# Edge sums of the last three node tiles by accumulating indirect DMAs, the order check taken out of the head, and the half blocks moved forward

## The chip, the cores and the metric

The kernel runs on one core of one Trainium2 chip. The metric is the device time of one launch in microseconds (us). One core has five engines that run side by side and wait for each other by semaphores: TensorE (PE, with its weight loads shown apart as PEld), VectorE (DVE), ScalarE (ACT), GpSimd (POOL) and SyncE (SP). SP issues nearly all plain DMAs; POOL issues the indirect ones, whose rows are picked by a list of indices in on-chip memory.

## The reference, cut to what matters

There are 3125 nodes with 256 features and 103,125 directed edges, sorted by destination: each of 50,000 drawn pairs in both directions, and a loop on each node. A node so has about 33 incoming edges.

```python
xn = layernorm(x)
agg = segment_sum(xn[src], dst, num_segments=N)          # the edge sums
h = relu(agg @ W_rel + b_rel + xn @ W_root)
gates = h @ W_ih.T + b_ih + b_hh                         # i, f, g, o; f is not used
h_lstm = sigmoid(o) * tanh(sigmoid(i) * tanh(g))
x = x + h_lstm @ W_fc + b_fc + mix(xn)                   # mix: 8 heads, linear attention
x = x + moe(layernorm(x))                                # 8 experts, top 2, 256 -> 1024 -> 256
```

## The kernel before, in words

The nodes are cut into T = 25 tiles of P = 126 rows. The kernel is one long program with stages that overlap a little.

**Head.** `norm` normalizes the nodes in five batches and stores them in `xn_dram`; `root` makes xn @ W_root for seven groups of tiles (`CUTS`). Beside it the generator `find` looks up the edges. Nodes are grouped by D = 6 (NG = 525 groups, GQ = 5 columns of GP = 105). For each group, five scans over the firsts of 128-edge rows (L258) and two rounds of indirect DMAs (`near` L266, `both` L281) bring its 256 edge slots; DVE turns them into a key (target within the group and source tile) and a row (source within its tile); L305 and L306 check that the edges are sorted, a matmul with ones (L311) adds up what is `wrong`, and `off`, made from that, is added to the keys (L325) so that nothing matches if the check fails. Then `rowT` and `keyT` hold the lists turned by PE.

**Edge stage.** The 3150 target columns are cut into chunks of AC = 252 (twelve, and a last one of 126). For each chunk, `build` makes an adjacency block from the lists: DVE compares (L382: `hr` and `hk`), PE multiplies the one-hot pairs (L388), ACT copies out (L390), 18 columns a step, 14 steps (`bank`) a chunk. Then 100 matmuls (L671: 25 source tiles, two halves of features, `hi` and `lo` parts of xn) sum the neighbours into `aggT`, which ACT copies at L679. While chunk c is multiplied, the blocks of chunk c+1 are built. The dictionary `queue` hangs the steps of the mixer (`fetch`, `means`, `differences`, `squares`, `sums`, `normed`, `products`) behind given banks, batch b from chunk 2b on. SP clears `xs_dram` in four fills (L698), after chunks 0, 2, 4 and 6. After the edge stage, `tc.If(total > 0)` holds a slow path for unsorted or overfull edges, which isn't entered with these inputs.

**Node stage.** `chunk(t0, t1, pending)` takes three or four tiles at a time: `aggT` by W_rel (L951), the gates (L961, 12 groups of matmuls for each of four m), W_fc (L980), then the router. POOL adds the bias to `base` (L943) and scatters the rows to their experts' lists in `xs_dram` by indirect DMAs (L1092, "puts"), 8 for a chunk of four tiles. The router's end of one chunk (`pending`) is issued behind m = 1 of the next.

**Block stage.** 24 sure blocks of SB = 256 slots and HSURE = 4 half blocks of 128 go through the experts' two matmuls (L865, L889). Each block loads 2 MB of weights into two buffers. For a block, POOL gathers the output rows (`old`, L845), adds (L900) and scatters them back (L901); a gather waits for the scatters of the block before it, since they may touch the same rows. The list `jobs` sets the order; half blocks stand behind blocks 10, 14, 18 and 22:

```python
        for b in range(EARLY, SURE):
            jobs.append((b, False))
            if b >= NE and (b - NE) % HSURE == HSURE - 2:
                jobs.append(((b - NE) // HSURE, True))
```

The order on each engine is set by a scheduler from the program's order; `tc.issue_after(ins)` places what is written under it behind that instruction.

Of the kernel before, what the change touches and what calls it, by code (L numbers as in the profile page):

```python
# [17 lines left out]
N = 3125  # L18
# [18 lines left out]
D = 6  # L37
NG = NP // D
GQ = 5
GP = NG // GQ  # L40
SB = 256
# [24 lines left out]
def gps_layer(  # L66
# [61 lines left out]

    aggT = main.tile([128, KC, NP], F32, name="aggT")
    edges = ExitStack()  # L130
# [17 lines left out]
    raw = sp.tile([128, 2, NCP], I32, name="raw")  # L148
    firsts = sp.tile([GP, NCP], I32, name="firsts")

    behind = sp.tile([128, NCP], I32, name="behind")
    nc.vector.memset(behind[96:, :], FAR)
    wroot = gw.tile([128, KC, DH], F32, name="wroot")

# [4 lines left out]

    nc.sync.dma_start(firsts, dst[0:1, :].to_broadcast([GP, NCP]))  # L160
    nc.sync.dma_start(raw[:, 0, :], dst)
    nc.sync.dma_start(raw[:, 1, :], src)
    def load_batch(b):
# [16 lines left out]
    nc.gpsimd.iota(limit, pattern=[[D * GP, GQ]], base=0, channel_multiplier=D,  # L180
                   allow_small_or_imprecise_dtypes=True)
    ones = const.tile([128, 128], F32, name="ones")
    nc.vector.memset(ones, 1.0)
# [36 lines left out]
    def find():  # L220
# [33 lines left out]

        below = sp.tile([GP, GQ], F32, name="below")
        scr = sp.tile([GP, NCP], F32, name="scr", tag="ends", bufs=3)
        for q in range(GQ):
            nc.vector.tensor_scalar(scr, firsts, limit[:, q:q + 1], None, op0=OP.is_lt, op1=OP.add,  # L258
                                    accum_out=below[:, q:q + 1])
# [11 lines left out]
        for q in range(GQ):  # L271
            nc.vector.tensor_scalar(scr[:, :128], near[:, q, :, 0], limit[:, q:q + 1], None,
                                    op0=OP.is_lt, op1=OP.add, accum_out=below[:, q:q + 1])
# [13 lines left out]
        st_ = sp.tile([GP, GQ, GE], F32, name="st_", tag="near")  # L287
        full = sp.tile([128, GQ], F32, name="full")
        nc.vector.memset(full, 0.0)
        for q in range(GQ):  # L290
            nc.vector.tensor_scalar(key[:, q, :], key[:, q, :], limit[:, q:q + 1], None,
                                    op0=OP.subtract)
            nc.vector.tensor_scalar(st_[:, q], g_src[:, q], -(P - 1) / 2.0, 1.0 / P,
                                    op0=OP.add, op1=OP.mult)
            nc.vector.tensor_scalar(st_[:, q], st_[:, q], MAGIC, MAGIC, op0=OP.add, op1=OP.subtract)
            nc.vector.scalar_tensor_tensor(g_src[:, q], st_[:, q], -float(P), g_src[:, q],
                                           op0=OP.mult, op1=OP.add)
            nc.vector.tensor_scalar(full[:GP, q:q + 1], key[:, q, GE - 1:], D - 0.5, None,
                                    op0=OP.is_lt)
            nc.vector.scalar_tensor_tensor(key[:, q], key[:, q], float(T), st_[:, q],  # L300
                                           op0=OP.mult, op1=OP.add)

        wrong = const.tile([128, 2], F32, name="wrong")
        order = sp.tile([128, NCP], F32, name="order", tag="ends", bufs=3)
        nc.vector.tensor_tensor(order, raw[:, 0, :], behind, OP.is_gt)  # L305
        nc.vector.tensor_reduce(wrong[:, 0:1], order, AX.X, OP.add)  # L306

        pins.append(nc.vector.tensor_reduce(wrong[:, 1:2], full, AX.X, OP.add))
        yield
        pw = ps_tr()  # L310
        nc.tensor.matmul(pw[:, :2], ones, wrong, start=True, stop=True)  # L311
        total_f = const.tile([128, 1], F32, name="total_f")
        nc.vector.tensor_reduce(total_f, pw[:, :2], AX.X, OP.add)
        off = const.tile([128, 1], F32, name="off")
        nc.vector.tensor_scalar(off, total_f, 1.0, float(FAR), op0=OP.min, op1=OP.mult)
        nc.vector.tensor_copy(total_i, total_f)
        for q in range(GQ):
            pt = ps_tr()
            for o, of in enumerate((g_src, key)):
                for h in range(GH):  # L320
                    nc.tensor.transpose(pt[:, (o * GH + h) * GP:(o * GH + h + 1) * GP],
                                        of[:, q, h * 128:h * 128 + 128], ident[:GP, :GP])
            nc.scalar.copy(rowT[:, q * GP:(q + 1) * GP, :],
                           pt[:, :GH * GP].rearrange("p (h g) -> p g h", h=GH))
            key_ = nc.vector.tensor_scalar(  # L325
                keyT[:, q * GP:(q + 1) * GP, :],
                pt[:, GH * GP:2 * GH * GP].rearrange("p (h g) -> p g h", h=GH),
                off, None, op0=OP.add)
        pins.append(key_)


# [61 lines left out]

    cuts = [*range(0, NP, AC), NP]
    chunks = list(zip(cuts, cuts[1:]))
# [55 lines left out]
    then(evacs[-1], rounded, 4)  # L451
    found.close()

    parts = builds(A0, 0)
    for c, n, m in ((5, 3, 4), (6, 3, NB)):
        root(c, lambda: [next(parts) for _ in range(n)])
        for _ in range(m):
            next(parts, None)
    with tc.issue_after(pins.pop().ins):
        for b in range(T // TB):  # L460
            u = slice(b * TB, b * TB + TB)
            nc.vector.tensor_tensor(lo[:, u, :], xn[:, u, :], hi[:, u, :], OP.subtract)
    nodes.close()

    gl = ctx.enter_context(tc.tile_pool(name="gl", bufs=1, side="right"))
# [99 lines left out]
    def squares(b, h):  # L565

        if h == 0:
            dn = mp.tile([P, TB, KC, 132], F32, name="dn", bufs=1)
            nc.gpsimd.memset(dn[:, :, :, 128:], 1.0)
            std = stat.tile([P, nh, 1], F32, name="hstd", bufs=2)  # L570
# [67 lines left out]

    queue = {}
    nb_ = T // TB  # L640
    for b in range(nb_):
        for c, i, step, *of in (
# [3 lines left out]
                (3, 1, products)):  # L646
            queue.setdefault((2 * b + c, i), []).append((step, b, *of))

    with tc.tile_pool(name="odd", bufs=1) as op_:
        As = [A0, op_.tile([P, T, AC], F32R, name="A1")]  # L650
        for c, (d0, d1) in enumerate(chunks):
# [5 lines left out]
            def bank(i):  # L657
# [3 lines left out]
                with ExitStack() as queued:  # L661
                    for ins in built:
                        queued.enter_context(tc.issue_after(ins.ins))
                    for step, *of in queue.pop((c, i), ()):
                        step(*of)

            i = 0
# [12 lines left out]
            if c == 1:  # L680
# [6 lines left out]
                for load in loads:  # L687
                    tc.add_manual_dep(load.ins, last.ins.name, mybir.DependencyInfo(
                        mybir.DependencyClass.Sync, mybir.DependencyReason.DATA), reason="later")
            if c == 2 * nb_ + 1:  # L690
                mixed()
# [13 lines left out]

    total = nc.values_load(total_i[0:1, 0:1], min_val=0, max_val=128 * NCP + NG)
    with tc.If(total > 0):
        with tc.tile_pool(name="any", bufs=1) as ap_:
# [8 lines left out]
            with tc.For_i(0, NCP, 1) as g:  # L717
# [33 lines left out]
                    in_=sums, in_offset=None, compute_op=OP.add)  # L751
            for t0 in range(0, T, TQ):
                ts = range(t0, min(T, t0 + TQ))
                ag = ap_.tile([P, TQ, C], F32, name="ag")
                nc.sync.dma_start(ag[:, :len(ts), :], tiles_of(agg_dram, t0, t0 + len(ts)))
                for k in range(KC):
# [4 lines left out]
                    col = aggT[:, k, t0 * P:(t0 + len(ts)) * P]  # L761
                    nc.vector.tensor_tensor(col, pt[:, :len(ts) * P], col, OP.add)

# [4 lines left out]
    class Block:  # L768


        def __init__(self, b, fp, half=False, xs=None):
# [21 lines left out]
            if xs is None:  # L793
                xs = fp.tile([128, NH, ROW], F32, name="xs", bufs=4)[:, :self.nh, :]
                rows = nc.sync.dma_start(xs, xs_b.rearrange("(h p) c -> p h c", p=128))
# [38 lines left out]
        def fetched(self, early):  # L834
# [4 lines left out]
            with ExitStack() as queued:  # L839
# [4 lines left out]
                for h in range(self.nh):  # L844
                    get = nc.gpsimd.indirect_dma_start(  # L845
                        out=old[:, h, :], out_offset=None, in_=out[:most, :],
                        in_offset=self.rows_(h), bounds_check=most - 1, oob_is_err=False)
                    for put in written if early else (*written, *ends_of_base):
                        after(get, put)
# [4 lines left out]
        def parts(self, following=None, apart=False):  # L854
# [21 lines left out]
            for h in range(nh):  # L876
# [11 lines left out]
                for m in range(KF):  # L888
                    mm = nc.tensor.matmul(po, hf[:, m, 128 * h:128 * h + 128], self.w2[:, m, :],  # L889
                                          start=(m == 0), stop=(m == KF - 1))  # L890
                y = fp.tile([128, C], F32, name="y", bufs=2 if early else 4)
                nc.vector.tensor_tensor(y, po, self.b2s, OP.add)  # L892
# [36 lines left out]
    with tc.tile_pool(name="gnn", bufs=1) as hp, tc.tile_pool(name="rt", bufs=2) as rp:  # L929
        CT = TQ * P  # L930
        wrows = rp.tile([P, NE, C], F32, name="wrows", bufs=1)
        nc.sync.dma_start(wrows, wr_dram[None, :, :].to_broadcast([P, NE, C]))

        def chunk(t0, t1, pending):

            ts = range(t0, t1)
            nt = len(ts)
            n = nt * P
            tok = slice(t0 * P, t0 * P + n)

# [6 lines left out]
            for m in range(KH):  # L947
                ms = slice(128 * m, 128 * m + 128)
                pm = ps_mm()
                for k in range(KC):  # L950
                    nc.tensor.matmul(pm[:, :n], wrel[:, k, ms], aggT[:, k, tok],  # L951
                                     start=(k == 0), stop=(k == KC - 1))
# [3 lines left out]
            for m in range(KH):  # L956
# [12 lines left out]
                if m == 1:  # L969

                    with tc.issue_after(mm.ins):
                        for _ in pending:
                            pass
            yield
            xl = rp.tile([P, TQ, C], F32, name="xl")
# [255 lines left out]
    with tc.tile_pool(name="ffn", bufs=2) as fp:  # L1231

        jobs = []
        for b in range(EARLY, SURE):
            jobs.append((b, False))
            if b >= NE and (b - NE) % HSURE == HSURE - 2:
                jobs.append(((b - NE) // HSURE, True))
        now = Block(jobs[0][0], fp, jobs[0][1])
# [89 lines left out]
```

## Time and profile before

| | us |
|---|---|
| runs shown (3) | 1113.99, 1111.55, 1114.54; median 1113.99 |
| profiled execution, its own time | 1118.92 |
| its span, first to last instruction | 1117.1 |
| PE busy | 1049.5 (94%) |
| PE weight loads busy | 814.8 (73%) |
| DVE busy | 553.6 (50%) |
| ACT busy | 437.9 (39%) |
| POOL busy | 245.3 (22%) |
| mean granted TensorE clock | 0.977 |

The profile page lists busy times and groups of instructions: line, engine, operation, output and inputs, count, busy time, mean duration, and the idle time just before them with what ended it. Matmuls overlap in the pipeline, so the duration of one is longer than the distance to the next. The trace can also be asked for instructions in order of time, and for busy times in given windows; those answers give starts in us from the span's start. The profiled execution is 4.93 us above the median of the runs shown.

### The profile page before, as it was taken

To read this page: it belongs to the slowest core of one execution; us is meant where nothing else is said; L and a number is where in the kernel's file an instruction comes from. 1 tells how busy PE (TensorE), PEld (TensorE's weight loads), DVE (VectorE), ACT (ScalarE), POOL (GpSimd) and SP (SyncE) were. 2 spreads that over 40 slices of the span, in tenths; PEclk is the share of its full clock that TensorE was granted. 3 is DMA by queue.
4 is the path that set the end of the run, shared out by engine and by line. 5 is a ranking of instruction groups with operands and counts; after the bars stand their busy time and mean duration, and the time that the engine had idled before them with its cause. 6 is when DMAs were issued, how large, how long until landed. Compare 5 with 4: busy or idle time off the path is not lost. (4 is left out here: it accounts for less than half of the span.)

```text
span 1117.1 us, 15758 instructions
## 1 busy us (share of the span) xinstructions
PE 1049.5 (94%) x5620; PEld 814.8 (73%) x5620; DVE 553.6 (50%) x1760; ACT 437.9 (39%) x942; POOL 245.3 (22%) x290
## 2 busy tenths in 40 slices
PE   4789999999999999999999999999999999999991
PEld 2358989989998454545465656788888888888881
DVE  5667778688772148484848644472112222222210
ACT  4454746647641334242435334452222322222230
POOL 2110000000000101212121130344434434344353
PEclk8999999999999999999999999999999999999996
DMA  8842897956003211262122310147666766676740
GB/s 252 314 165 80 223 289 180 242 146 169 1 1 113 74 37 62 69 222 63 51 58 60 97 59 15 48 130 268 202 220 213 248 209 207 217 242 202 244 163 26
DMA packets 113583, 164.28 MB, mean 147 GB/s; under 512 B 8102, under 2 KB 95945, under 8 KB 113370
## 3 DMA queue, kind: packets, MB, share of 16 engines
q1 hardware_dynamic: 103584, 140.49, 40.7%
q0 software_dynamic: 9072, 21.87, 5.9%
q8 instruction: 47, 0.77, 0.3%
q10 hardware_dynamic: 840, 0.83, 0.2%
q14 instruction: 40, 0.33, 0.1%
HBM read 104.98 MB, written 59.06 MB: 147 GB/s over the span
## 5 line engine op out<-in xcount | busy, mean ns | idle before, releaser
L961 PE MATMUL ps_mm<-hT,wih 128*128 128x504 f32 (+1 forms) x672 | 260.2, 548 | 0.0
L961 PEld LDWEIGHTS ps_mm<-hT,wih 128*128 128x128 f32 x672 | 128.3, 192 | 127.7 <-issue 91.5
L865 PE MATMUL ps_mm<-xe,w 128*128 128x256 f32 (+1 forms) x896 | 185.3, 364 | 0.0
L889 PE MATMUL ps_o<-w,hf 128*128 128x256 f32 x832 | 184.9, 379 | 0.0
L671 PE MATMUL ps_o<-A,hi 126*128 126x252 f32 (+1 forms) x650 | 178.1, 307 | 0.0
L865 PEld LDWEIGHTS ps_mm<-xe,w 128*128 128x128 f32 x896 | 160.5, 190 | 20.2 <-issue 0.2
L889 PEld LDWEIGHTS ps_o<-w,hf 128*128 128x128 f32 x832 | 155.7, 190 | 19.9
L671 PE MATMUL ps_o<-A,lo 126*128 126x252 f32 (+1 forms) x650 | 162.7, 283 | 0.0
L867 ACT ACTIVATE hf<-ps_mm,sm 128x256 f32<-128x256 f32 (+1 forms) x160 | 72.7, 454 | 184.4 <-PE ps_mm L865 181.4
L390 ACT CAST A<-ps_mm 126x450 fp32r<-126x450 f32 x175 | 93.9, 539 | 104.0 <-PE ps_mm L388 102.4
L671 PEld LDWEIGHTS ps_o<-A,hi 126*128 126x128 f32 x650 | 126.4, 194 | 1.8 <-ACT aggT L679 1.7
L671 PEld LDWEIGHTS ps_o<-A,lo 126*128 126x128 f32 x650 | 126.6, 195 | 0.0
L382 DVE TENSOR_TENSOR hr<-two,rowT 128x756 bf16<-128x756 bf16 x175 | 95.9, 548 | 49.8 <-PE ps_mm L388 49.0
L388 PE MATMUL ps_mm<-hk,hr 128*126 128x150 bf16 x1050 | 103.7, 235 | 15.2 <-DVE hk L382 15.1
L382 DVE TENSOR_TENSOR hk<-two,keyT 128x900 bf16<-128x900 bf16 x175 | 108.9, 622 | 0.0
L388 PEld LDWEIGHTS <-hr 128*126 128x126 bf16 x1050 | 92.5, 139 | 21.0 <-DVE hk L382 19.4
L963 ACT ACTIVATE act<-ps_mm,bg 128x504 f32<-128x504 f32 (+1 forms) x84 | 53.1, 636 | 111.2 <-PE ps_mm L961 101.2
L892 DVE TENSOR_TENSOR y<-ps_o,b2s 128x256 f32<-128x256 f32 x52 | 22.1, 424 | 118.9 <-PE ps_o L889 72.6
L1092 POOL DMA_INDIRECT xs_dram<-rows,at_i x50 | 50.2, 1003 | 122.6 <-DVE at_i L1090 108.6
L1012 DVE SCALAR_TENSOR_TENSOR scr<-xl,wrows 126x256 f32<-126x256 f32 x152 | 72.3, 476 | 3.1
L845 POOL DMA_INDIRECT old<-out_dram,xs x52 | 53.8, 1034 | 84.8 <-issue 51.4
L943 POOL TENSOR_TENSOR base<-base,bfc 126x1024 f32<-126x1024 f32 (+1 forms) x7 | 15.4, 2208 | 235.8 <-DMA base<-in_x_dram 154.2
(265 smaller groups left out, 1049.8 us busy)
## 6 DMA issues: line engine op xcount, KB each, us to landing
w<-in_W_dram SPq DMA_DIRECT2D x56, 1024.0 KB
xs_dram<-blank SPq DMA_DIRECT2D x3, 7022.5 KB
xs_dram<-blank SPq DMA_DIRECT2D x1, 6757.5 KB
xs<-xs_dram SPq DMA_DIRECT2D x21, 265.0 KB
root_dram<-hr SPq DMA_DIRECT2D x8, 504.0 KB
root<-root_dram SPq DMA_DIRECT2D x4, 1008.0 KB
b2s<-in_b_dram SPq DMA_DIRECT2D x28, 128.0 KB
xn_dram<-xn SPq DMA_DIRECT2D x5, 630.0 KB
```

Source lines behind the costliest of these rows:

```text
L382: row = nc.vector.tensor_tensor(to[:, :m], two[:, :, :w, :].to_broadcast([128, m, w, GH]), of[:, g:g + m, None, :].to_broadcast([128, m, w ...
L388: mm = nc.tensor.matmul(pa[:P, i * DT:(i + 1) * DT], hr[:, i, :, h], hk[:, i, :, h], start=(h == 0), stop=(h == GH - 1))
L390: copy = nc.scalar.copy(A[:, :, c0:c0 + m * D], pa[:P, :m * DT].rearrange("p (d t) -> p t d", t=T))
L671: last = nc.tensor.matmul(pg[k][:, :n], of[:, t, 128 * k:128 * k + 128], A[:, t, :n], start=(t == 0 and of is hi), stop=(t == T - 1 and of ...
L845: get = nc.gpsimd.indirect_dma_start(out=old[:, h, :], out_offset=None, in_=out[:most, :], in_offset=self.rows_(h), bounds_check=most - 1, ...
L865: mm = nc.tensor.matmul(pm, self.w1[:, k, 128 * m:128 * m + 128], self.xe[:, k, :], start=(k == 0), stop=(k == KC - 1))
L867: nc.scalar.activation(hf[:, m, :], pm, AF.Gelu, bias=b1s[:, m:m + 1])
L889: mm = nc.tensor.matmul(po, hf[:, m, 128 * h:128 * h + 128], self.w2[:, m, :], start=(m == 0), stop=(m == KF - 1))
L961: mm = nc.tensor.matmul(pm[:, :n], wih[:, k, i, 128 * m:128 * m + 128], hT[:, k, :n], start=(k == 0), stop=(k == KH - 1))
L963: nc.scalar.activation(act[:, i, :n], pm[:, :n], AF.Tanh if gate == 2 else AF.Sigmoid, bias=bg[:, gate, m:m + 1])
L1012: nc.vector.scalar_tensor_tensor(scr, xl[:, i, :], 1.0, wrows[:, e, :], op0=OP.mult, op1=OP.mult, accum_out=lg[:, i, e:e + 1])
L1092: put = nc.gpsimd.indirect_dma_start(out=xs_dram[:, :], out_offset=bass.IndirectOffsetOnAxis(ap=at_i[:, i:i + 1], axis=0), in_=rows[:, i, ...
```

## The change

Four things are done together.

1. The edge sums of the last three tiles (TG = 3, 378 target columns) are no longer made by matmuls. The edge stage ends after 11 chunks of 252 (TA = 22 tiles), and `find` serves 480 groups in 4 columns of 120. A new generator `find_last` finds, for each node of the last three tiles, its first edge and up to J = 60 sources, in the same manner as `find`; slots that aren't the node's point at row N of `xn_dram`, which holds zeros. `adds` then issues 60 x 3 indirect DMAs, each of which adds 126 rows of `xn_dram` onto one tile's sums in `flat` on chip. Adds onto the same tile wait for one another. 81 of them stand on POOL's queue in the edge stage (from chunk 0, bank 11, on; 5 for every 8 banks), 99 in the node stage, 5 behind each m. `turned`, behind m = 2 of the chunk that ends at tile 22, transposes the sums by PE for the last chunk.
2. The check of the order, its matmul and `off` move from `find` to `find_last`; `off` goes into the sources instead of the keys. `find_last` runs in chunk 0: its scans behind the last build of the first block, the rest behind banks 4, 8 and 10.
3. The mixer's batches start at chunks 0, 2, 3, 5 and 6 instead of 0, 2, 4, 6 and 8, and the `dn` memset goes from POOL to DVE.
4. The half blocks stand behind blocks 4, 7, 10 and 13. `xs` has 5 buffers instead of 4, `y` 6 instead of 4, and the gathers join the group of DMAs that are ordered by hand only.

```diff
-NG = NP // D
-GQ = 5
-GP = NG // GQ
+TG = 3
+TA = T - TG
+GQ = 4
+GP = 120
+NG = GQ * GP
+JE = 64
+J = 60
...
-    aggT = main.tile([128, KC, NP], F32, name="aggT")
+    aggT = main.tile([128, KC, TA * P], F32, name="aggT")
+    flat = main.tile([128, TG * C], F32, name="flat")
+    acc = flat[:P].rearrange("p (m c) -> p m c", c=C)
+    accT = flat[:, :KC * TG * P].rearrange("p (k n) -> p k n", k=KC)
...
-        order = sp.tile([128, NCP], F32, name="order", tag="ends", bufs=3)
-        nc.vector.tensor_tensor(order, raw[:, 0, :], behind, OP.is_gt)
-        nc.vector.tensor_reduce(wrong[:, 0:1], order, AX.X, OP.add)
...
-        nc.tensor.matmul(pw[:, :2], ones, wrong, start=True, stop=True)
...
+    def find_last():
+        below = ep.tile([P, TG], F32, name="below2")
+        for m in range(TG):
+            scr = sp.tile([128, NCP], F32, name="scr2", tag="ends", bufs=3)
+            nc.vector.tensor_scalar(scr[:P], firsts[:P], node[:, m:m + 1], None, op0=OP.is_lt,
+                                    op1=OP.add, accum_out=below[:, m:m + 1])
...
+        for m in range(TG):
+            nc.gpsimd.indirect_dma_start(
+                out=near[:, m].rearrange("p e o -> p (e o)"), out_offset=None,
...
+        nc.vector.tensor_tensor(order, raw[:, 0, :], behind, OP.is_gt)
+        nc.vector.tensor_reduce(wrong[:, GQ:GQ + 1], order, AX.X, OP.add)
+        yield
...
+        for m in range(TG):
+            nc.vector.tensor_scalar(mine[:, m], both[:, m, :, 0], node[:, m:m + 1], None,
+                                    op0=OP.is_equal)
...
+        nc.tensor.matmul(pw[:, :GQ + 2], ones, wrong, start=True, stop=True)
...
+        nc.vector.tensor_scalar(mine, mine, float(N), off[:P], op0=OP.add, op1=OP.add)
+        nc.vector.tensor_scalar(source, mine, float(N), None, op0=OP.min)
+
+    def adds():
+        nc.gpsimd.memset(acc, 0.0)
+        for j in range(J):
+            for m in range(TG):
+                yield nc.gpsimd.indirect_dma_start(
+                    out=acc[:, m, :], out_offset=None, in_=xn_dram[:, :],
+                    in_offset=bass.IndirectOffsetOnAxis(ap=source[:, m, j:j + 1], axis=0),
+                    compute_op=OP.add)
...
-    cuts = [*range(0, NP, AC), NP]
+    cuts = range(0, TA * P + 1, AC)
...
-    for b in range(nb_):
+    queue = {(0, i): [(next, last_steps, None)] for i in (4, 8, 10)}
+    ADDS = 11
+    for b, c0 in enumerate((0, 2, 3, 5, 6)):
...
+                n = c * NB + i - ADDS
+                if n >= 0 and n * 5 // 8 > (n - 1) * 5 // 8:
+                    next(adding)
...
+        def turned():
+            for _ in adding:
+                pass
+            pts = [ps_tr() for _ in range(KC)]
+            for k in range(KC):
+                for m in range(TG):
+                    nc.tensor.transpose(pts[k][:, m * P:(m + 1) * P],
+                                        acc[:, m, 128 * k:128 * k + 128], ident[:P, :P])
+            for k in range(KC):
+                nc.scalar.copy(accT[:, k, :], pts[k][:, :TG * P])
...
+                for i in range(5):
+                    add = next(adding, None)
+                    if add is not None and i == 0:
+                        after(add, mm)
+                if m == 2 and t1 == TA:
+                    with tc.issue_after(mm.ins):
+                        turned()
...
-            if b >= NE and (b - NE) % HSURE == HSURE - 2:
-                jobs.append(((b - NE) // HSURE, True))
+            if (b - EARLY) % 3 == 1 and (b - EARLY) // 3 < HSURE:
+                jobs.append(((b - EARLY) // 3, True))
```

## The prediction

> **What bounds the kernel now.** I read the page's first two parts, then busy times with one window for each edge chunk (a chunk ends where ACT starts the first copy to `aggT`, L679: 116.2, 134.6, 157.5, 178.2, 200.6, 221.5, 242.9, 263.5, 286.0, 306.9, 326.7, 344.1, 355.5 us), then DVE and POOL in order of time.
>
> ```profile
> span 1117.1 us, 15758 instructions
> PE 1049.5 (94%) x5620; PEld 814.8 (73%) x5620; DVE 553.6 (50%) x1760; ACT 437.9 (39%) x942; POOL 245.3 (22%) x290
> PE   4789999999999999999999999999999999999991
> DVE  5667778688772148484848644472112222222210
> POOL 2110000000000101212121130344434434344353
> ```
>
> PE is the bound from slice 4 to the last; POOL is empty in slices 4 to 13, the edge stage, where DVE runs close behind PE.
>
> ```profile
> L388 PE MATMUL ps_mm<-hk,hr 128*126 128x150 bf16 x1050 | 103.7, 235 | 15.2 <-DVE hk L382 15.1
> ...
> core 0: us, PE busy (x) PEld busy (x) DVE busy (x) ACT busy (x) POOL busy (x), PEclk, DMA share, GB/s
> 116.20:134.60 18.40, 18.40 (x187) 18.14 (x186) 14.96 (x30) 15.96 (x56) 0.00 (x0) 1.00 1.03 270
> 134.60:157.50 22.90, 20.49 (x186) 19.71 (x185) 19.68 (x37) 9.53 (x20) 0.00 (x0) 0.93 1.08 287
> 157.50:178.20 20.70, 20.70 (x208) 20.49 (x206) 14.49 (x28) 16.13 (x57) 0.13 (x1) 1.00 1.12 281
> 306.90:326.70 19.80, 19.00 (x186) 18.16 (x185) 17.44 (x35) 9.50 (x20) 0.00 (x0) 1.00 0.01 2
> 326.70:344.10 17.40, 17.40 (x164) 17.20 (x164) 7.03 (x18) 4.46 (x10) 0.00 (x0) 1.00 0.00 1
> 344.10:355.50 11.40, 11.40 (x104) 11.40 (x102) 2.34 (x10) 0.65 (x3) 0.00 (x0) 1.00 0.49 183
> ```
>
> These are chunks 1, 2, 3, 10, 11 and 12. With nothing but builds and `differences` a chunk takes 18.4; with `products` 20.7, PE full; with `squares`, `sums`, `normed` and the next `means` 22.9, PE idle 2.4 beside DVE's 19.7; the same without `means` 19.8; with 7 builds and `products` 17.4; the half-wide one without builds 11.4.
>
> **The matmuls taken away.** Chunks 1 to 12 take 355.5 - 116.2 = 239.3. After the change there are chunks 1 to 10, and with the new starts of the batches each holds: 1 differences 18.4; 2 squares and means 22.9; 3 products and means 20.9; 4 squares 20.5 (19.8, and ACT now has differences too); 5 products, squares and means 23.5 (22.9, products mostly inside DVE's excess); 6 products 20.9; 7 squares 20.5; 8 products and squares 21.7; 9 products 20.6; 10 neither builds nor steps, 100 matmuls about 0.117 apart, 11.7. Sum 201.6: **-37.7**. Bounds -32 (0.8 more in seven mixed chunks) and -41 (mixed chunks at PE's own 20.7). The node stage multiplies the same columns, so nothing changes on PE there.
>
> **The search moved into chunk 0.**
>
> ```profile
> 5.31 1.05 DVE L258 TENSOR_SCALAR_CACHE_REDUCE scr<-firsts,limit 105x808 f32<-105x808 int32 x1 [3.07 <-DMA firsts<-in_dst_dram]
> ...
> 24.93 0.35 DVE L272 TENSOR_SCALAR_CACHE_REDUCE scr<-near,limit 105x128 f32<-105x128 f32 x1 [2.55 <-DMA near<-ends_dram,at_i]
> ...
> 51.80 1.01 DVE L305 TENSOR_TENSOR order<-raw,behind 128x808 f32<-128x808 int32 x1
> ...
> 66.03 0.16 DVE L313 TENSOR_REDUCE total_f<-ps_tr 128x1 f32<-128x2 f32 x1 [9.32 <-PE ps_tr L311]
> ```
>
> The order check leaves the head for nothing: after it DVE idled 9.32 for PE. What the head does lose on PE is the matmul L311 (0.3) and 4 of 20 list transposes (3.0 in all, so 0.6): **-1**, bounds 0 and -1.5. In chunk 0 DVE gains three scans at 1.10, order 1.0 and its reduce 0.9, two small casts 0.3: 5.5 in one piece, ahead of the first build for chunk 1; behind bank 4 three counts and one sum, 1.4; behind bank 8 three compares and a reduce, about 0.9 by the 0.35 of L272; behind bank 10 sums and sources, about 1.5. Together 9.3. DVE was free for 24.2 - 19.8 = 4.4 of 92.0 to 116.2, so 4.9 come out on PE. Three waits are new: DVE for `near2`, for `both2` and for its matmul on PE. All later builds queue behind them on DVE, and PE behind the builds. Banks come every 1.45 or so; a gather of three needs 2.7 of issue and 2.5 to 6.8 of landing (below) where four banks give 5.8. I take 2.1: **+7**, bounds +3 (scans inside the 2.64 that DVE idled at 99.25, waits hidden) and +13 (nothing hidden).
>
> **The adds.** No accumulating DMA ran before, so bounds come from plain indirect ones.
>
> ```profile
> 18.10 1.16 POOL L266 DMA_INDIRECT near<-ends_dram,at_i  x1 [1.02 <-DVE xn L336]
> ...
> 444.01 1.10 POOL L1092 DMA_INDIRECT xs_dram<-rows,at_i  x1 [15.87 <-DVE at_i L1090]
> 445.42 1.00 POOL L1092 DMA_INDIRECT xs_dram<-rows,at_i  x1 [0.30 <-issue]
> ...
> 1091.70 1.05 POOL L845 DMA_INDIRECT old<-out_dram,xs  x1 [2.26 <-issue]
> 1092.74 0.54 POOL L843 MEMSET old<- 128x512 f32 x1
> 1094.18 0.72 POOL L900 TENSOR_TENSOR old<-y,old 128x256 f32<-128x256 f32 x1 [0.89 <-DMA old<-out_dram,xs]
> ```
>
> Issues follow each other at 1.3. From issue to the waiting instruction, a gather takes 2.5 on a quiet queue (1091.70 to 1094.18) and 6.8 on a loaded one (18.10 to 24.93). Three adds to three tiles are in flight and the fourth waits for the first, so a round of three costs the larger of 3.9 and the landing: 3.9 below; above, 6.8 doubled for the second operand that an add must read, 13.6. I take 5, nearest the quiet rows, since from 265 on the queues are nearly empty. What can it wait for? 27 rounds stand in the edge stage, from about 115 to its end near 325: room for 7.8 each. In the node stage 33 rounds share POOL with `base` (2.2, L943) and 8 puts (10.4) for each 56.2 us chunk; PE's m steps pace them, a put waits until some 30 into the chunk for DVE's `at_i`, and 14 adds, 4.7 rounds, must fit from 41 to the next chunk's first m, 73: again 7 or so, and 40 us are spare before `turned`. So up to 7.5 a round the adds cost **0**; they hide beside PE. Beyond that PE stands at `turned`: 33 rounds times the excess, some 25 to 30 us for each us of landing.
>
> A rule that speaks against this: the puts above were issued every 1.3 while DVE was busy 35.7 of 56.2, longest 1.373 of 50, so I see no stop. The Trainium skill, "SBUF — State Buffer", "Who interferes with whom" and "A bandwidth-pool intuition that's wrong", holds that POOL can't write a DMA's descriptors while DVE works in a mode that takes their shared ports, and gives 3.1 us against 0.62 for such a DMA. If each issue took 3.1, a round would take 9.3 and the whole gain be lost.
>
> `turned` adds six transposes; eight records of that kind took 1.03 (41.57, L356), so twelve take **+1.5**, bounds 1.5 and 4 (wait for two PSUM buffers); the ACT copies (0.5 each) have a node chunk's end to hide in. For packets of the adds among fills and loads, and DVE's `dn` memset now waiting for `products`, I set **+2**, bounds 0 and +10 (a `q` load late behind a fill).
>
> **Half blocks.** PE takes 14.25 for a full block and 10.7 for a half wherever it stands, PE was never idle from 750 on, and weights keep coming at a DMA share of 0.7. The end can move: the last matmul ended at 1094.6, the last scatter was issued at 1106.5, since each gather waits for the block before. With the half block gone from the place before last, two full blocks' time of PE lets the chain catch up: from the scatter at 1078.3 to that at 1088.4 a full block took 10.1 against 14.25. But a half took 6.8 against 7.5, so little is won at the end: **0**, bounds -8 and +4. More `xs` and `y` buffers only allow more lag.
>
> **Sum.** -37.7 - 1 + 7 + 1.5 + 2 = -28.2. Span 1117.1 to 1089, the profiled execution's 1118.9 to 1090.7; that execution was 4.9 above the median, so the median 1114.0 goes to 1085.8.
>
> **Rivals.** (a) *The adds land late.* An add may read, sum and write back row by row. At 9 a round instead of 7.5, PE waits some 40 at `turned`: 1126, slower than before; it decides from about 8.5 on. For it: the doubled loaded row. Against: 2.5 quiet, and little traffic in the node stage. 0.11. (b) *DVE takes the bound in the edge stage.* Chunk 0 grows by 13 and mixed chunks wait for batches that now overlap: -32 + 13 + 1.5 + 8 - 1 = -10, so 1103; for it DVE's 19.7 of 22.9 in chunk 2. 0.16. (c) *The tail shortens too*: -8 beside the forecast, 1078. 0.12. (d) *The removal doesn't reach the end*, because the block stage, fed by the same gathers, takes it back: 1112. For it: 11.9 us of chain behind the last matmul; against: PE was never idle there. 0.03. The forecast has 0.58.
>
> **Numbers.** A measurement tells some 0.3%, 3.3 us. Range 1072 (c, and the better edge bound) to 1108 (b with its bounds); outside stay (a) and some of (d). Faster 0.86, same 0.03, slower 0.11, from (a).
>
> **What would show it.** Right: 11 L679 pairs, the last near 323; POOL busy with adds every 1.3 to 2 in threes; no PE idle before the six transposes; the node stage's chunks still 56.2. Wrong: PE idle there with a DMA onto `flat` as releaser; more DVE waits before L388's successor than 15.1; chunk 0 beyond 129.

## The result, and the profile after

The kernel after takes 1246.96 us (median of 4 runs, 1237.64 to 1257.0) against 1112.82 before: a ratio of 1.117, 95% interval [1.111, 1.123]. By the medians it is slower by 134 us. The ratio counts the fast runs alone and so leaves out the longest, 1257.0, which is the profiled execution, with a span of 1255.0. The page of after, the same rows as shown of before, and the groups of the adds (L394) and of the gate matmuls (L1052, L961 before):

```profile
span 1255.0 us, 15252 instructions
PE 1036.3 (83%) x5296; PEld 788.6 (63%) x5296; DVE 534.9 (43%) x1733; ACT 424.3 (34%) x918; POOL 559.7 (45%) x471
PE   4787999999789994693791760799999999999995
POOL 2104556677663344445435436602543343344444
L394 POOL DMA_INDIRECT flat<-xn_dram,source x180 | 309.4, 1719 | 319.3 <-DMA flat<-xn_dram,source 281.8
L1052 PE MATMUL ps_mm<-hT,wih 128*128 128x504 f32 (+1 forms) x672 | 274.1, 568 | 134.0 <-ACT act L1054 132.2
```

PE is busy 13.2 us less, but stands idle for 219 us of the span (68 before), two thirds of it in slices 16 to 26. POOL waited 281.8 us between its adds for an earlier add to land. Cut into stages (edge stage; the gap until the first gate matmul; node stage; block stage; the tail from the last matmul on), the profile shows where the loss lies. These are the gap and the node stage, first before, then after:

```profile
core 0: us, PE busy (x) PEld busy (x) DVE busy (x) ACT busy (x) POOL busy (x), PEclk, DMA share, GB/s
355.70:364.40 8.70, 7.09 (x16) 3.05 (x17) 2.10 (x5) 2.06 (x5) 0.00 (x0) 1.00 0.44 152
364.40:714.80 350.40, 345.87 (x1072) 193.31 (x1071) 194.06 (x808) 133.09 (x216) 63.51 (x56) 0.99 0.23 71
...
331.80:354.20 22.40, 8.82 (x17) 3.71 (x17) 2.12 (x5) 2.27 (x5) 15.72 (x10) 0.71 0.71 148
354.20:860.90 506.70, 360.68 (x1078) 198.98 (x1077) 195.16 (x808) 133.01 (x217) 221.12 (x155) 0.85 0.34 73
```

The lengths of these stages in all profiled executions, each read off in the same way (gap: last edge matmul to first gate matmul):

| kernel | edge stage ends | gap | node stage | block stage | tail | span |
|---|---|---|---|---|---|---|
| before | 355.7 | 8.7 | 350.4 | 379.8 | 22.5 | 1117.1 |
| after | 331.8 | 22.4 | 506.7 | 379.8 | 14.3 | 1255.0 |
| no adds (e1) | 330.8 | 8.4 | 351.1 | 379.7 | 14.3 | 1084.3 |
| order mended (e2) | 328.2 | 21.2 | 355.7 | 379.9 | 14.1 | 1099.1 |
| plain gathers (e3) | 330.2 | 8.6 | 437.2 | 379.8 | 14.5 | 1170.3 |
| before + half blocks (e4) | 354.5 | 8.0 | 347.2 | 379.8 | 15.6 | 1105.1 |
| 65 edge adds (e5) | 328.4 | 8.5 | 373.2 | 379.8 | 14.6 | 1104.5 |
| six tiles (e6) | 331.8 | 8.4 | 375.3 | 379.7 | 12.0 | 1107.2 |
| edge adds only (e7) | 330.1 | 15.5 | 349.5 | 379.7 | 12.0 | 1086.8 |
| three rows buffers (e8) | 331.5 | 13.9 | 493.6 | 380.1 | 14.3 | 1233.4 |
| six tiles, late sum (e9) | 332.0 | 8.4 | 351.5 | 379.8 | 13.4 | 1085.1 |
| 97 edge adds (e10) | 336.4 | 8.5 | 351.5 | 379.8 | 14.2 | 1090.4 |
| no waits for PE (e11) | 329.4 | 23.7 | 459.6 | 379.8 | 14.4 | 1206.9 |

From before to after: edge stage -23.9, gap +13.7, node stage +156.3, tail -8.2. Who waits in the node stage of after, from the lists of what DVE and PE waited for (engine, tile and line, releaser; us in total, times, longest):

```profile
DVE rows L1179 <- DMA xs_dram<-rows,at_i: 151.8, 4, 50.5
PE ps_mm L1052 <- ACT act L1054: 132.2, 4, 45.3
```

Four times DVE stood at the first write to a chunk's `rows` buffer, whose scatters (L1191, of the chunk two before) had not been issued. DVE's next gate product queues behind that, then ACT's, then PE: one case, in order of time on all engines:

```profile
488.72 1.59 POOL L394 DMA_INDIRECT flat<-xn_dram,source  x1 [0.30 <-issue]
490.62 1.04 POOL L1191 DMA_INDIRECT xs_dram<-rows,at_i  x1 [0.30 <-issue]
...
502.62 0.17 DVE L1179 COPY rows<-token 126x4 int32<-126x4 int32 x1 [33.24 <-DMA xs_dram<-rows,at_i]
...
509.31 0.68 DVE L1057 TENSOR_TENSOR act<-act 128x504 f32<-128x504 f32 x1
...
510.56 0.67 ACT L1054 ACTIVATE act<-ps_mm,bg 128x504 f32<-128x504 f32 x1
...
511.27 5.59 PE L1052 MATMUL ps_mm<-hT,wih 128*128 128x504 f32 x8 [27.32 <-ACT act L1054]
```

POOL issued its scatters without a pause once it came to them; it came late, because the adds ahead of them were slow. This is POOL in the node stage of after:

```profile
383.96 1.59 POOL L394 DMA_INDIRECT flat<-xn_dram,source  x1 [3.13 <-DMA flat<-xn_dram,source]
388.33 1.59 POOL L394 DMA_INDIRECT flat<-xn_dram,source  x1 [2.78 <-DMA flat<-xn_dram,source]
390.22 1.59 POOL L394 DMA_INDIRECT flat<-xn_dram,source  x1 [0.30 <-issue]
394.49 1.59 POOL L394 DMA_INDIRECT flat<-xn_dram,source  x1 [2.68 <-DMA flat<-xn_dram,source]
399.06 1.62 POOL L394 DMA_INDIRECT flat<-xn_dram,source  x1 [2.98 <-DMA flat<-xn_dram,source]
403.32 1.59 POOL L394 DMA_INDIRECT flat<-xn_dram,source  x1 [2.65 <-DMA flat<-xn_dram,source]
```

An add every 4.3 to 4.6 us, one in flight, and only the first of each five without a wait for its predecessor. The DMA packets say the same: the add issued at 394.49 has its last packet at 398.29, and the next is issued at 399.06. The order of the instructions on POOL, as built (a, b, c are adds onto the three tiles, P is a scatter, base the bias addition), shows why:

```
edge stage:  a b c a b c a b c ...
node stage:  b c b b base base a a a a a c c c c c b b b b b a a a a a base
             c c c c c b P P P P P P P P b b b a b a a a a c c c c c base ...
```

In the node stage five adds onto one tile stand in a row. Of the five behind an m only the first waited for a matmul; the scheduler was free to place the other four elsewhere (e2 takes that freedom away). With three tiles in turn, the adds that wait are onto a, c and b by turns, and from one of them up to the next onto the same tile lie five adds of that tile. Adds onto one tile must wait for one another, so there POOL pays the whole round trip each time.

### The profile page after: what moved, and what is told of

Its sections match the earlier page's. It is cut to its first block, busy times and chain, and to the rows that moved or that the text cites. A ratio compares the mean times of both kernels' runs of the same rounds, so it can differ in the third digit from the quotient of the medians.

```text
span 1255.0 us, 15252 instructions
## 1 busy us (share of the span) xinstructions
PE 1036.3 (83%) x5296; PEld 788.6 (63%) x5296; DVE 534.9 (43%) x1733; ACT 424.3 (34%) x918; POOL 559.7 (45%) x471
## 3 DMA queue, kind: packets, MB, share of 16 engines
q0 software_dynamic: 38080, 45.57, 18.6%
## 5 line engine op out<-in xcount | busy, mean ns | idle before, releaser
L394 POOL DMA_INDIRECT flat<-xn_dram,source x180 | 309.4, 1719 | 319.3 <-DMA flat<-xn_dram,source 281.8
L1052 PE MATMUL ps_mm<-hT,wih 128*128 128x504 f32 (+1 forms) x672 | 274.1, 568 | 134.0 <-ACT act L1054 132.2
L1052 PEld LDWEIGHTS ps_mm<-hT,wih 128*128 128x128 f32 x672 | 133.1, 201 | 274.4 <-ACT act L1054 136.5
L746 PE MATMUL ps_o<-A,hi 126*128 126x252 f32 x550 | 151.3, 307 | 0.6 <-ACT A L458 0.6
L746 PE MATMUL ps_o<-A,lo 126*128 126x252 f32 x550 | 138.0, 283 | 0.0
L458 ACT CAST A<-ps_mm 126x450 fp32r<-126x450 f32 x154 | 82.3, 538 | 85.7 <-PE ps_mm L456 81.5
L746 PEld LDWEIGHTS ps_o<-A,hi 126*128 126x128 f32 x550 | 106.5, 194 | 2.4 <-ACT aggT L754 1.3
L746 PEld LDWEIGHTS ps_o<-A,lo 126*128 126x128 f32 x550 | 106.7, 194 | 0.0
L456 PE MATMUL ps_mm<-hk,hr 128*126 128x150 bf16 x924 | 91.8, 235 | 16.1 <-DVE hk L450 15.7
L450 DVE TENSOR_TENSOR hk<-two,keyT 128x900 bf16<-128x900 bf16 x154 | 95.7, 622 | 0.0
L1058 ACT ACTIVATE act<-act 128x504 f32<-128x504 f32 (+1 forms) x28 | 16.2, 578 | 186.3 <-DVE act L1057 186.3
L980 POOL TENSOR_TENSOR old<-y,old 128x256 f32<-128x256 f32 x52 | 37.7, 725 | 86.4 <-DMA old<-out_dram,xs 62.4
```

The costliest lines, as they stand in the source:

```text
L394: yield nc.gpsimd.indirect_dma_start(out=acc[:, m, :], out_offset=None, in_=xn_dram[:, :], in_offset=bass.IndirectOffsetOnAxis(ap=source[: ...
L450: row = nc.vector.tensor_tensor(to[:, :m], two[:, :, :w, :].to_broadcast([128, m, w, GH]), of[:, g:g + m, None, :].to_broadcast([128, m, w ...
L456: mm = nc.tensor.matmul(pa[:P, i * DT:(i + 1) * DT], hr[:, i, :, h], hk[:, i, :, h], start=(h == 0), stop=(h == GH - 1))
L458: copy = nc.scalar.copy(A[:, :, c0:c0 + m * D], pa[:P, :m * DT].rearrange("p (d t) -> p t d", t=T))
L746: last = nc.tensor.matmul(pg[k][:, :n], of[:, t, 128 * k:128 * k + 128], A[:, t, :n], start=(t == 0 and of is hi), stop=(t == T - 1 and of ...
L980: nc.gpsimd.tensor_tensor(old[:, h, :], y, old[:, h, :], OP.add)
```

## The experiments

Theory A: the adds cause the loss, through POOL's queue; A1: through their order on it. Rivals B to L are named in the expectations.

**e1, without adds.** In `adds`:

```diff
-        for j in range(J):
+        for j in range(0):
```

> The 180 adds are left out, so the last three tiles' edge sums are zero; all else of the change stays (find_last, turned, the shorter edge stage, the half blocks). Theory A (the adds cause the whole loss, as POOL's queue): the time falls to what the recorded sum gives without them, 1080 to 1092 us, with node chunks of 56 us and no wait of DVE for the scatters' rows buffer. Rival B (find_last, the mixer's overlapped batches or the half blocks cost much of it): more than 1115 us.

Measured: 1085.24 us, ratio 0.973 [0.971, 0.976] to before. The adds cost 162 us, more than the whole loss; B falls. The rest of the change is worth 29.5 us (before took 1114.72 beside this run).

**e2, the order mended.** Behind an m:

```diff
-                    if add is not None and i == 0:
+                    if add is not None:
                         after(add, mm)
```

> All five adds behind an m wait for its matmul, not the first alone, so that the queue goes round the three tiles again; in the kernel after, its node stage has five adds onto one tile in a row. Theory A1 (the order on the queue makes each add wait out the round trip of the one before, 4.3 us each, and the scatters behind them come late): rounds of three fall from about 13 us to about 6, the waits of DVE for rows in the node stage (152 us) go to below 15, and the time falls to 1095 to 1115 us, with the wait of 12 to 18 us at the start of the node stage left. Rival C (an accumulating DMA is slow in itself, whatever its neighbours): rounds stay above 10 us and the time above 1200 us.

Measured: 1104.40 us, 0.992 [0.988, 0.995]: 143 us less than after by one condition. POOL's queue goes a b c again, and its node stage looks like this, beside the lines of after above:

```profile
373.00 1.59 POOL L394 DMA_INDIRECT flat<-xn_dram,source  x1 [0.30 <-DMA flat<-xn_dram,source]
374.89 1.59 POOL L394 DMA_INDIRECT flat<-xn_dram,source  x1 [0.30 <-issue]
376.79 1.59 POOL L394 DMA_INDIRECT flat<-xn_dram,source  x1 [0.30 <-issue]
378.68 1.79 POOL L394 DMA_INDIRECT flat<-xn_dram,source  x1 [0.30 <-issue]
```

A round of three takes 5.7 to 6.6, set by issue and by PE's pace; no wait for `rows` is left among the longest of the node stage. A1 holds, C falls. Of the 19 us to e1, 12.8 of the profiled spans are the gap before the gates.

**e3, plain gathers in the order of after.** `compute_op=OP.add` is dropped.

> The same 180 DMAs at the same places, but each overwrites its tile instead of adding (the sums are then only the last rows). Theory A1: the chain is made of issue and round trip, of which the packets' own 1.4 us is the smaller part; the time falls by at most 0.5 us for each of 99 adds, to 1195 to 1247 us. Rival C: an overwriting gather lands in 2.5 us or less after its issue as on the quiet queue of before; rounds fall below 8 us and the time to 1100 to 1130 us.

Measured: 1172.69 us, 1.052 [1.049, 1.054], between the two forecasts. An overwriting gather's issue is 1.00 against 1.59, and the adds of the node stage come every 3.9 instead of 4.6 us in the median; DVE still waits 85.7 for `rows`. So adding costs 0.6 of POOL's time for each DMA and nothing that can be seen in landing; the chain remains. The two runs differ in more than the adding, though: the plain gathers move the same bytes in fewer packets (20,800 on that queue against 38,080). POOL is also past the edge stage's 81 in time here (gap 8.6). A1's bound of 0.5 for each was too low, and it left the gap out.

**e4, the half blocks alone**, on the kernel before: the changed condition in `jobs`, `xs` bufs 5, `y` bufs 6 and the line with the group of gathers.

> The kernel before with nothing but the half blocks moved forward (behind blocks 4, 7, 10, 13), five xs buffers, six y buffers and the gathers in the hand-ordered group. The recorded prediction: no change, 1106 to 1118 us. Rival D (the block stage gains by it, as the kernel after's block stage is 394 us long against 404): 1102 to 1106 us, the last scatter nearer to the last matmul or the block stage's PE idle time smaller.

Measured: 1107.21 us, 0.993 [0.990, 0.996], some 7.5 below the 1114.72 of before beside it. The block stage is as long as ever; the tail is 15.6 instead of 22.5, and the last scatter is issued 4.8 after the last matmul instead of 11.9. The time lies within the 1106 to 1118 that the recorded "no change" allowed and just above D's 1102 to 1106, but a gain there is: D's sign of it, a last scatter nearer to the last matmul, came true; the block stage itself gains nothing.

**e5, fewer adds ahead of the conditional block**, on e2:

```diff
-                if n >= 0 and n * 5 // 8 > (n - 1) * 5 // 8:
+                if n >= 0 and n * 4 // 8 > (n - 1) * 4 // 8:
...
-                for i in range(5):
+                for i in range(6 - m % 2):
```

> As the run with the order mended (all five adds wait for the matmul), but 65 adds instead of 81 stand before the conditional block, and 115 behind it, 6 and 5 by turns behind an m. Theory F (after the conditional block every engine waits until POOL has come past its own part of it, so PE waits for POOL's backlog of adds): with POOL there before PE, the gap between the last edge matmul and the first gate matmul falls from 21 us to 8 or 9, as without adds, and the time from 1104 to 1090 to 1097 us. Rival G (the node stage can't carry 16 more adds; they come out again as late scatters or at the six transposes): 1100 us or more.

Measured: 1107.13 us, 0.993 [0.991, 0.996]. F's gap came true (8.5), its time did not: as G has it, the node stage takes the gain back and is 17.5 longer than in e2. The last of the 115 adds was issued at 649.0 (636.8 in e2) and the transposes of `turned` waited, in PE's waits of e5:

```profile
PE ps_tr L1021 <- DMA flat<-xn_dram,source: 6.7, 3, 3.7
```

That is 6.7 of the 17.5. PE's other waits in that stage make up 12.6 against 6.9 in e2, and some 5 us more of busy time go with a granted clock of 0.968 against 0.983; why those waits grew is left open.

**e6, six tiles**, on e2:

```diff
-                    out=acc[:, m, :], out_offset=None, in_=xn_dram[:, :],
+                    out=(acc, acc2)[j % 2][:, m, :], out_offset=None, in_=xn_dram[:, :],
...
             for _ in adding:
                 pass
+            nc.vector.tensor_tensor(acc, acc, acc2, OP.add)
```

> As the run with the order mended, but even and odd source columns go to two sets of three tiles, so that six adds are in flight; one DVE addition joins the sets ahead of the transposes. Theory H (in the edge stage a round waits for landing, about 7 us beside the fills, not for POOL's issue of 1.9): three adds then take about 5.7 to 6.5 us instead of 8.5, POOL is past its 81 adds before the edge stage ends, and the time falls to 1086 to 1096 us. Rival I (beside the fills the DMA engines are full and set the pace): rounds stay near 8 us, the gap before the gates stays, 1100 to 1107 us.

Measured: 1111.85 us, 1.000 [0.998, 1.002]. H's cause was right (three adds take 6.1 in the edge stage, the gap is 8.4, I falls), its time was not: a new wait took the gain, in DVE's order of time in e6:

```profile
602.27 0.18 DVE L215 BATCH_NORM_AGGREGATE mv<-bn 126x2 f32<-126x6 f32 x1
626.10 0.96 DVE L1021 TENSOR_TENSOR flat<-flat,flat 126x768 f32<-126x768 f32 x1 [23.64 <-DMA flat<-xn_dram,source]
```

The added sum had no tie to the matmul that `turned` stands behind; it was placed early on DVE's queue and held everything behind it until the last add landed.

**e7, the edge stage's adds alone**: `range(0)` behind each m on e2, and `turned` draws no more.

> The 81 adds of the edge stage alone; the 99 of the node stage are left out, so the last tiles' sums are incomplete. If the two prices add up (theory F for the edge stage's part), this stands 12 to 13 us above the run without adds: 1096 to 1100 us, with the gap of 21 us before the gates. If the gap comes from the adds behind the conditional block, it is gone: 1085 us.

Measured: 1088.06 us, 0.975 [0.970, 0.981], so 3 us above e1, not 12. The gap was 15.5 in this execution: POOL issued its 81st add at 340.1 against 343.9 in e2, and the edge stage ended 1.9 later. So the gap is the edge adds', as large as POOL is late; of the 16 us between e7 and e2, some 6 are this difference and 6 lie in the node stage.

**e8, three `rows` buffers in the kernel after** (one `y` buffer less for the early blocks).

> The kernel after with its order of adds as it is, but three buffers for the router's rows instead of two (and one y buffer less for the three early blocks, to make room). Theory A2 (POOL's queue is simply too long for the node stage: some 80 adds at 4.4 us and 20 at 1.9, 50 scatters at 1.3 and 15 us of base make some 470 us against 357): the time stays at 1225 to 1255 us, the wait only moves, from DVE's rows to the next buffer or to the transposes. Rival J (the two rows buffers couple DVE to POOL, the queue would have had room): below 1190 us.

Measured: 1239.28 us, 1.113 [1.104, 1.121]. The waits of PE in e8's node stage:

```profile
PE ps_tr L1021 <- DMA flat<-xn_dram,source: 86.7, 3, 78.7
PE ps_mm L1042 <- DVE hT L1044: 26.9, 2, 23.4
PE ps_mm L1052 <- ACT act L1054: 22.3, 1, 22.3
```

The time stays and most of the wait moves, now to the transposes (DVE still waits 28.2 for `rows`): POOL's queue is the bound there (A2), not the buffers (J).

**e9, e6 with the sum tied down, and e10, that with 97 adds in the edge stage** (`n * 6 // 8`):

```diff
-            nc.vector.tensor_tensor(acc, acc, acc2, OP.add)
+            after(nc.vector.tensor_tensor(acc, acc, acc2, OP.add), mm)
```

> The run with six tiles, with the one DVE addition of the two sets told to wait for the same matmul as the transposes; there it stood far ahead on DVE's queue and held DVE for 23.6 us at 602. Theory K (that wait alone ate the gain of the six tiles): the node stage loses its stall of 22 us, and the time falls from 1112 to 1087 to 1093 us. Rival L (the adds of the node stage end too late for the transposes whoever waits for them): PE waits 10 us or more at the addition or the transposes, 1098 us or more.

> The same with 97 adds in the edge stage and 83 behind it. If POOL is past 97 adds before the edge stage ends (they need about 2 us each from 125 on, so until 320): as the kernel with 81, or 1 to 3 us less, 1085 to 1092 us. If not, the gap before the gates comes back by 2 us for each add that is late: 1092 to 1100 us.

Measured: e9 1088.38 us, 0.979 [0.975, 0.982]; e10 1087.82 us, 0.977 [0.974, 0.980]. K holds: the stall of 22 is gone, and all 180 adds cost 3 us over none by the medians, 6 by the ratios to before. POOL's idle time ahead of L394 in e9 names what is left of the waits:

```profile
  issue: 49.9, 164
  PE ps_mm L1056: 13.7, 8
...
  DMA flat<-xn_dram,source: 0.6, 2
```

Of the 281.8 us that POOL waited for landings in after, 0.6 remain. Moving 16 more adds forward changed nothing that can be told. Both kernels beat before and after, by some 25 and 159 us.

**e11, no wait of an add for PE** (the `after(add, mm)` and its condition are dropped from the kernel after):

> The kernel after without any wait of an add for a matmul: the scheduler then keeps the three tiles in turn (as in the run with the order mended), but places all 99 adds of the node stage ahead of the first chunk's scatters on POOL's queue. If it was the succession on one tile alone that cost, rounds are 6 us and the time is that of the mended order, 1100 to 1110 us. If what counts is when POOL comes to the scatters (theory A as a whole), the adds last until some 550 us, the first scatters start there instead of near 440, and DVE waits for its rows buffer from the third chunk on, some 60 to 90 us: 1150 to 1190 us.

Measured: 1209.17 us, 1.088 [1.084, 1.092]. The tiles go in turn and rounds take 5.7 for the most part, but all 99 adds stand ahead of the first chunk's scatters, which are issued at 565.20. DVE's longest wait in e11:

```profile
DVE rows L1176 <- DMA xs_dram<-rows,at_i: 109.8, 1, 109.8
```

So a good order among the adds is not enough: what counts is when POOL comes to the scatters. The wait was longer than the 60 to 90 expected, and the time is above the 1150 to 1190.

## Why the prediction failed, step by step

**The edge matmuls: right.** Chunks 1 to 10 took 203.4 us in after (the first copy to `aggT` at 128.2, the last at 331.6) against 201.6 in the sum; without adds (e1) they took 202.1, and the +2 set for the adds' packets covers the rest.

**`find_last`: right; the head: wrong by some 4.** From the first edge matmul to the end of chunk 0 it is 26.7 against 20.4, so +6.3 for the +7 set. But the first edge matmul came at 101.5 against 95.8 (100.6 without adds) where the sum had -1. Part of this is spread between executions: the eleven kernels with this head have it at 97.7 to 101.5, 100.2 in the median, and e4, with the head of before, at 97.7. The waits of PE for ACT's `xt` and for `xn` are longer by 2 to 3 and by 1 us; why is left open.

**`turned`: right.** The node stage of e1 is 351.1 against 350.4. The six transposes take 0.8 us in after (806.8 to 807.6), not the 1.5 that was set for twelve records.

**The half blocks: mis-sized.** Set at 0, they are worth 8.2 in the tail, rival (c)'s figure (7.5 alone, in e4): the chain of scatters does catch up behind the last half block. (A half takes PE 7.5 us, as the prediction says in its last comparison, not the 10.7 that it gives first.) This and the head's error have opposite signs, so it was in part luck that the sum without adds, 1085.8, met e1's 1085.2.

**The adds: the step that failed.** "Three adds to three tiles are in flight and the fourth waits for the first, so a round of three costs the larger of 3.9 and the landing ... I take 5." Three things were wrong in it.

First, in flight. That holds in the edge stage. In the node stage one add is in flight, a round is three round trips of 4.3 to 4.6, some 13 us, as the order of the built kernel shows; the prediction counted the adds on POOL's queue and didn't look at their tiles. The price that the prediction put on a late round was sound: a round of 13.2 is 5.7 over the room of 7.5, and at its 25 to 30 us for each us that makes 143 to 171; the node stage grew by 156. Rival (a) had this form with another cause (an add that reads, sums and writes row by row), which e2, e3 and e11 refute, and at 9 a round too small a size.

Second, the place. The prediction had PE wait at `turned`. The scatters stand in the same queue behind the adds, and DVE's `rows` needs them first; e8 shows `turned` next in line.

Third, the conditional block, which the prediction passes over. In the edge stage a round took 8.5, not 5 (81 adds from 122.9 to 351.5), over the room of 7.8 for each, so POOL was late. The adds landed 6.8 after issue in the median: mostly 3.6 to 4.3 where no fill ran, 6 to 11 beside the fills. The prediction took 5 because "from 265 on the queues are nearly empty", but in after the last fill moved from 258 to 287, and 48 of the 81 adds were issued before 265. In order of time around the block's end in after:

```profile
333.44 5.31 PE L1042 MATMUL ps_mm<-aggT,wrel 128*128 128x504 f32 x12 [1.61 <-DVEq L782]
...
349.90 1.59 POOL L394 DMA_INDIRECT flat<-xn_dram,source  x1 [0.30 <-DMA flat<-xn_dram,source]
349.98 1.86 DVE L1044 TENSOR_TENSOR hT<-ps_mm,root 128x504 f32<-128x504 f32 x3 [17.78 <-DMA flat<-xn_dram,source]
350.72 3.73 PE L1042 MATMUL ps_mm<-aggT,wrel 128*128 128x504 f32 x4 [11.97 <-DVE hT L1044]
```

DVE's first instruction behind the block goes on as POOL issues its 81st add, the last ahead of the block. So it does in e2, e7, e8 and e11, where POOL is late too: between 0.6 before and 2.4 after the start of that issue. In e3, e5, e6, e9 and e10 POOL is early, DVE waits there about as long as without adds, and the gap is 8.4 to 8.6. So the engines behind the block wait until POOL has passed. That they do so because the block also uses indirect DMAs is argued from the kernel; no run isolates it.

**The rule that spoke against the change** was weighed rightly. L394 took 1.59 in the median and 1.72 in the mean; in the edge stage, beside a busy DVE, 5 of 81 issues took over 3 us (the longest 4.71), and all 180 together only 25 us more than at the shortest. The Trainium skill, "SBUF — State Buffer", "Who interferes with whom", says that POOL is blocked for as long as a DVE instruction in a two-port mode holds the ports that the two share. That may explain those five; no run here isolates it, and it did not decide.

## What to carry to other kernels

Before a chain of DMAs is called hidden, write down the built order of its queue and look at what each entry depends on: a tie on one of five instructions lets the scheduler rearrange the other four, and three in flight became one. Count the queue's whole length against the stage (adds, scatters, element-wise work), and look for who needs the entries behind: scatters that free a buffer, or a conditional block that everybody passes. When a fix removes a wait and the time stays, look for the next one: e5 and e6 each removed the gap and lost its 13 us again further on, and one more line gave them back (e9).

## What the runs showed of the hardware

An accumulating indirect DMA of 126 rows of 1 KB lands 3.65 us after its issue begins when the queue is quiet (issued at 374.97 in after, last packet at 378.62), and adding costs 1.59 of POOL instead of 1.00, while its packets take no longer than a plain gather's (1.3 to 1.6 us for the 126 rows against 1.1 to 1.8, in the quiet parts of after and e3).

After a pause PE is slow. In PE's order of time in after, the first 8 gate matmuls behind the 27 us pause took 5.59 us (0.70 each), 48 later ones 20.53 (0.43 each):

```profile
511.27 5.59 PE L1052 MATMUL ps_mm<-hT,wih 128*128 128x504 f32 x8 [27.32 <-ACT act L1054]
519.39 20.53 PE L1052 MATMUL ps_mm<-hT,wih 128*128 128x504 f32 x48
```

The group's busy time is 274.1 in after against 260.3 in e1, so the pauses cost 14 us beyond their own length, and the mean granted clock is 0.920 against 0.983. Behind this pause it was 0.50 from 511.27 to 514.67, over the first four of the matmuls, and 1.00 from 516.86 on. The Trainium skill, "TensorE: Matmul & The Clock Gate", section "Part 1: The HAM clock gate (the "warmup" mystery)", says that an idle array runs at half its clock until it has been busy for about 3.4 us, which these rows fit.
